# A four-layer selective-scan stack on one core: table-set blocks of ScalarE placed only behind a lift, and the next chunk's prologue re-cut around them

## Chip, cores and metric

One Trainium2 chip, one of its cores. The metric is the device time of one execution of the whole program in microseconds. The kernel before takes 22061.91 us, the median of three runs (22050.39 to 22083.94).

## What is computed

An image batch of 4 x 64 x 64 tokens with 128 channels goes through four layers. Layers 0, 1 and 3 are state-space (Mamba-like) blocks over 256 inner channels and 16 states, layer 2 is a gated block. Cut to what matters:

```python
xn = _ln(x, n1w, n1b)
xx, z = jnp.split(xn @ in_w, 2)                  # 256 inner channels each
xc = _silu(depthwise_conv3x3(xx) + conv_b)
xs = rows, columns, rows reversed, columns reversed of xc         # k = 0..3
dts, Bs, Cs = split(x_proj_w[k] @ xs[k])         # 8, 16, 16 rows
delta = jax.nn.softplus(dt_w[k] @ dts + dt_b[k])
def step(h, t):                                  # 4096 positions, per k
    h = jnp.exp(d_t[..., None] * A) * h + (d_t * x_t)[..., None] * B_t
    return h, jnp.einsum('bkdn,bkn->bkd', h, C_t)
y = sum over k of (ys[k] + Ds[k] * xs[k]), put back into row order
x = x + (_ln(y, ow, ob) * _silu(z)) @ out_w
x = x + gelu(_ln(x, n2w, n2b) @ fc1 + fc1b) @ fc2 + fc2b
```

Layer 0 uses the exact gelu, layers 1 and 3 the tanh form. All data are 32-bit floats.

## The kernel before, in words

**Turns, chunks, periods.** A turn is one batch element in one of the three state-space layers: 12 turns. In a turn each of the four directions k walks over 4096 positions in 8 chunks of 512: 32 chunks to a turn, 384 in all. The 256 channels are two halves of 128 partitions, and the 16 states come in four groups q of four; a chunk is done in 8 periods i, each for one half m and one group q (`place`, L879). There are 3072 periods, written out one behind another in the loop at L985. Nothing reorders them: the order in which Python issues instructions is the order of each engine's queue.

**One period.** DVE runs four scans over 512 positions (`scan`, L918: h = da * h + db), two with db from PSUM and two with db made by DVE itself. In the order of issue:

- ACT: two exponentials `da` for the next period (`decay`, L903), a small `save` of the last state (L928), two more `da`, another `save`, then the **lift** (L915): it copies delta*x of the next period into one of two PSUM banks `dv`, and can do so only when the scan (i, side 1, j 0) has read that bank. Then four **diagonals** (L885), 128x128 each.
- DVE: scan, scan, the two multiplications of `dv` by a row of B (L1048, L1049), scan, scan. L1048 needs the lift that was issued in the period before.
- PE: `pair_db` (L895) for the next period, eight matmuls into the one PSUM tile `dbp`, which both first scans of the running period must have read; and `add_up` (L940), which sums the products h*C of the last period in PSUM.
- POOL: `times_c` (L934): h*C of two states in one 128x1024 multiplication, twice to a period, in even periods also their sum.
- SP issues the loads of the broadcast rows of B and C (`spread`, L870), every second period.

Buffers couple the engines: three `da` tiles, four `h` and four `hc` tiles, two `dv` banks, one `dbp` tile, one PSUM bank `misc` for the prologue, one PSUM bank `gap` for the work between layers.

**The prologue of the next chunk** (`prologue`, L814) is a generator that is advanced at ten of a chunk's 16 places. Place 2i (`piece(2 * i)`, L1040) lies in the middle of period i, behind `pair_db` and ahead of the second pair of `da`. Place 2i+1 (L1066) lies at the end of the period, behind lift, diagonals and `add_up`. `PIECES` (L37) lists the places. Before the change:

- 0: loads of xs and, backwards, of xd; 3: the two matmuls of `ps_x`; 4: copy to xd, `ps_dt` of the first half (L842)
- 6: ACT adds the bias to the first half (Identity, L845), `ps_dt` of the second half
- 8: Softplus of the second half (L845) and of the first (L847), then `natural_log_exp_and_others` is loaded again (L848); PE transposes B into `ps_bt` (L851)
- 9: xd is stored to memory, `bt` copied (L856), POOL forms delta*x of the first half (L859); 10: of the second half
- 11, 12, 13: delta*x transposed to `duT` (L865, L867), half by half

**The work between layers** (`between`, L231, and `combine`, L190) is a flat list of small steps: norms, the 3x3 convolution as nine matmuls with diagonal weights, projections, Silu (L461), Gelu (L528), stores. `other(number)` (L1008) is called four times in a period: number 0 behind the first scan, 1 in the middle behind `piece(2i)`, 2 behind the third scan (ahead of the lift on ACT), 3 at the end (behind the diagonals on ACT). Each call runs steps from the front of the list while less is done than is due; what is due grows with the place, and the steps' costs are counted in matmuls (`cost`, L78; `when`, L91). A call ends behind an `empty` step or where matmul steps and others meet. In the last and the first turn a few segments are `dense`: they count steps instead.

Softplus, Silu and Gelu each lie in another set of activation tables than the exponentials and logarithms. Each such block therefore loads a set, computes, and loads `natural_log_exp_and_others` again (L254, L848). ACT does nothing else in that time.

Of the kernel before, what the change touches and what calls it, by code (L numbers as in the profile page):

```python
# [14 lines left out]
AF = mybir.ActivationFunctionType  # L15
# [18 lines left out]
PAIRED = (0, 2, 4, 6)  # L34


PIECES = (0, 3, 4, 6, 8, 9, 10, 11, 12, 13)  # L37


_VSS = [  # L40
# [37 lines left out]
def cost(step):  # L78

    return getattr(step, "matmuls", 0) or (0.05 if step is empty else 0.25)  # L80


def empty():
# [7 lines left out]
def when(place):  # L91

    chunk, place = divmod(place - 1, 4 * len(ROOM))
    i, number = divmod(place, 4)
    return chunk + (sum(ROOM[:i]) + ROOM[i] * number / 4) / sum(ROOM)
# [3 lines left out]
def vss_stack_kernel(ctx: ExitStack, tc: tile.TileContext, x: bass.AP, weights, out: bass.AP, n_batch=B, layers=(0, 1, 2, 3)):  # L99
# [6 lines left out]
    nc = tc.nc  # L106
# [19 lines left out]
    for i in layers:  # L126
# [26 lines left out]
        at, end = VSS_AT["xp"]  # L153
# [77 lines left out]
    def between(e, frm, to, psums):  # L231
# [226 lines left out]

        def silu(c, of_z):

            def run():  # L461
                part = z.wide[:, 0 if of_z else 2 : 2 if c is None else 4]
                nc.scalar.activation(part, part, AF.Silu)
                tables()

            def turn(m):
                z.down = gap1.tile([P, W, RPC], F32, tag=("cen", "sq")[m], name="down")
                nc.scalar.copy(z.down, z.wide[:, 2 + m].rearrange("p (h w) -> p w h", w=W))

            def store(m):  # L470
                to_col = lane.x_col[:, m].rearrange("p (w h) -> p w h", h=H)
                nc.sync.dma_start(out=to_col[:, :, c * RPC : (c + 1) * RPC], in_=z.down)

            S.append(run)
            if c is not None:
                S.append(lambda: turn(0))
                later(lambda: nc.sync.dma_start(out=lane.x_row[:, :, cols(c)], in_=z.wide[:, 2:4]), 2)
                rest(1)
                S.extend((lambda: store(0), lambda: turn(1)))
                rest(1)  # L480
                S.append(lambda: store(1))
            elif of_z:
                rest()
# [24 lines left out]
        def mlp(c, store):  # L508
            def fresh():
                z.t = gap1.tile([P, CH], F32, tag="t", name="t")  # L510
                return z.t

            norm(lambda: z.res, fresh, v["n2w"], v["n2b"], eps5)
            for j in range(4):

                @tensor(1)
                def up(j=j):
                    if j == 0:
                        z.wide = gap1.tile([P, 4, CH], F32, tag="wide", name="hid")
                    z.ps = bank()  # L520
                    nc.tensor.matmul(z.ps, z.fc1[:, j * P : (j + 1) * P], z.t, start=True, stop=True)  # L521

                def take(j=j):
                    nc.scalar.activation(z.wide[:, j], z.ps, AF.Identity, bias=v["fc1b"][:, j : j + 1])

                S.extend((up, take))

            def gelu():  # L528
                nc.scalar.activation(z.wide, z.wide, v["gelu"])  # L529
                tables()  # L530

            S.append(gelu)
            rest(1 + breath)
            for j in range(4):

                @tensor(1)
                def down(j=j):
                    if j == 0:
                        z.ps = bank()
                    nc.tensor.matmul(z.ps, z.fc2[:, j, :], z.wide[:, j], start=(j == 0), stop=(j == 3))  # L540

                S.append(down)

            def add():
                nc.vector.scalar_tensor_tensor(z.res, z.ps, v["fc2b"], z.res, ALU.add, ALU.add)

            rest()
            S.append(add)
            rest(1)
            if store:  # L550
                later(lambda: nc.sync.dma_start(out=lane.res[:, cols(c)], in_=z.res))
# [257 lines left out]
    def scans(pool, ring, deep, psum):  # L809
# [4 lines left out]
        def prologue(s):  # L814


            lane, v = lanes[s.e % 2], s.v
            s.xs = ring.tile([P, 2, CH], F32, tag="xs", name="xs")
            nc.sync.dma_start(out=s.xs, in_=(lane.x_col if s.columns else lane.x_row)[:, :, cols(s.c)])
            if s.first:  # L820
                s.dt = pool.tile([R, DI], F32, tag="dt", name="dt_w")
                nc.sync.dma_start(out=s.dt, in_=weights[s.layer][1][:, s.k * DI : (s.k + 1) * DI])


            s.xd_d = lane.xd[s.k % 2][s.c]
            s.xd = pool.tile([2 * NX, CH], F32, tag="xd", name="xd")
            if s.back:
                nc.sync.dma_start(out=s.xd[:NX], in_=s.xd_d[1])
            yield
            if s.back:  # L830
                yield
            else:
                ps = psum.tile([P, CH], F32, tag="misc", name="ps_x")
                for m in range(2):
                    nc.tensor.matmul(ps[: 2 * NX], v["xp"][:, s.k % 2, m, :], s.xs[:, m], start=(m == 0), stop=(m == 1))
                yield
                nc.scalar.copy(s.xd, ps[: 2 * NX])
            s.delta = pool.tile([P, 2, CH], F32, tag="delta", name="delta")
            halves = (s.flip, 1 - s.flip)
            for m in halves:  # L840
                ps = psum.tile([P, CH], F32, tag="misc", name="ps_dt")
                nc.tensor.matmul(ps, s.dt[:, m * P : (m + 1) * P], s.xd[:R], start=True, stop=True)  # L842
                yield
                func = AF.Identity if m == halves[0] else AF.Softplus
                nc.scalar.activation(s.delta[:, m], ps, func, bias=v["dtb"][:, s.k, m : m + 1])  # L845
            m = halves[0]
            nc.scalar.activation(s.delta[:, m], s.delta[:, m], AF.Softplus)  # L847
            nc.scalar.preload_act_table_set("natural_log_exp_and_others")  # L848
            ps = psum.tile([P, 4, NX], F32, tag="misc", name="ps_bt")
            for j in range(4):  # L850
                nc.tensor.transpose(ps[:, j, :], s.xd[:NX, j * P : (j + 1) * P], ident[:NX, :NX])  # L851
            yield
            if not s.back:
                nc.sync.dma_start(out=s.xd_d.rearrange("k r t -> (k r) t"), in_=s.xd)
            s.bt = pool.tile([P, 4, N], F32, tag="bt", name="bt")
            nc.scalar.copy(s.bt, ps[:, :, R : R + N])  # L856
            s.du = pool.tile([P, 2, CH], F32, tag="du", name="du")
            for m in halves:
                nc.gpsimd.tensor_mul(s.du[:, m], s.delta[:, m], s.xs[:, m])  # L859
                yield  # L860
            s.duT = pool.tile([P, 4, 2, P], F32, tag="duT", name="duT")
            for m in halves:
                ps = psum.tile([P, 4, P], F32, tag="misc", name="ps_duT")
                for j in range(4):
                    nc.tensor.transpose(ps[:, j, :], s.du[:, m, j * P : (j + 1) * P], ident)  # L865
                yield
                nc.scalar.copy(s.duT[:, :, m, :], ps)  # L867
            yield
# [116 lines left out]
        for at, (s, i) in enumerate(periods):  # L985
            then = periods[at + 1] if at + 1 < len(periods) else None
            if i == 0:
                nxt = chunks[at // 8 + 1] if at // 8 + 1 < len(chunks) else None
                if nxt:
                    pro, nxt.dt = prologue(nxt), s.dt  # L990
                s.state = pool.tile([P, 2, N], F32, tag="state", name="state") if s.first else before[0].state
                if at % (8 * per_turn) == 0:
                    segments = [
                        SimpleNamespace(todo=steps, done=0, dense=True, total=len(steps), frm=frm, to=to)

                        if to - frm <= 4 * 8
                        else SimpleNamespace(
                            todo=steps, done=0, dense=False, total=sum(map(cost, steps)), frm=when(frm), to=when(to)
                        )
                        for steps, frm, to in meanwhile(s.turn)  # L1000
                    ]
# [6 lines left out]
            def other(number):  # L1008

                place = at % (8 * per_turn) * 4 + number  # L1010
                for g in segments:
                    gone = place if g.dense else when(place)
                    while g.todo and g.done < g.total * (gone - g.frm) / (g.to - g.frm):
                        step = g.todo.pop(0)
                        g.done += 1 if g.dense else cost(step)
                        step()

                        if gone < g.to and not g.dense and (step is empty or g.todo and not alike(step, g.todo[0])):
                            break
# [152 lines left out]
```

## Time and profile before

The profiled execution took 22072.22 us; its span, from the first to the last instruction, is 22070.4 us. The rest, 1.8 us, lies outside.

| What | Value |
|---|---|
| median of three runs | 22061.91 us |
| profiled execution, its span | 22072.22 us, 22070.4 us |
| a period, the span by 3072 | 7.184 us |
| a chunk, the span by 384 | 57.5 us |
| granted TensorE clock | 0.963 |
| table loads of Softplus (L845, L848) | 384 and 384, 1283 ns each |
| table loads of Silu (L463), of Gelu (L529), back again (L254) | 168, 96, 264, 1283 ns each |
| Softplus from PSUM, Softplus in place, 128x512 | 687 and 620 ns (medians) |
| Silu 128x1024, Gelu 128x2048 | 1057 and 1910 ns (medians) |

In the profile, PE is the matmuls and PEld the weight loads of TensorE, DVE VectorE, ACT ScalarE, POOL GpSimd, SP SyncE. A line such as "DVE dv L1048 <- ACT dv L916: 730.3, 328, 7.5" says that DVE sat idle ahead of its instruction at line 1048 until ACT's at line 916 ended: 730.3 us in total, 328 times, 7.5 us at most. In the timeline, the columns are start, duration, engine, line, operation, tiles and count; idle time ahead of the group and what ended it stand in brackets.

### The profile page before, as it was taken

How to read it: one execution, taken by the hardware profiler on the slowest of the kernel's cores; microseconds unless marked ns; L12 is line 12 of the kernel's file. 1: busy time of each engine (PE TensorE's matmuls, PEld its weight loads, DVE VectorE, ACT ScalarE, POOL GpSimd, SP SyncE). 2: the span in 40 equal slices, each digit the busy share in tenths (PEclk: the TensorE clock that was granted, in tenths of full speed). 3: DMA queues.
4: the chain of work that ended last, by engine and by line, in shares of the span. 5: the costliest groups of instructions: out<-in, count | busy, mean ns of one | idle time of the engine just before them, and what ended most of it. 6: DMA issues, size and time to landing. Idle time of an engine off the chain costs nothing. (4 is left out here: it accounts for less than half of the span.)

```text
span 22070.4 us, 216982 instructions
## 1 busy us (share of the span) xinstructions
PE 19694.9 (89%) x58234; PEld 10511.8 (48%) x58234; DVE 19479.8 (88%) x20186; ACT 18587.9 (84%) x40022; POOL 19266.5 (87%) x8862
## 2 busy tenths in 40 slices
PE   7898998898889889889989988989988988898897
PEld 3444444444444444444444444444444444444443
DVE  5999999999888888899889899989988888889996
ACT  6888888888888888888888888888888888888887
POOL 5999899899888888888889888988988888889996
PEclk9999999999999999999999999999999999999999
DMA  4444444444335434434534544444443453354342
GB/s 109 147 149 146 135 144 149 136 139 151 130 131 139 142 128 140 146 133 145 144 138 144 145 141 140 141 147 134 142 149 127 137 143 137 131 140 145 140 144 101
DMA packets 2437559, 3060.10 MB, mean 139 GB/s; under 512 B 1753840, under 2 KB 1790064, under 8 KB 2238192
## 3 DMA queue, kind: packets, MB, share of 16 engines
q1 hardware_dynamic: 2436336, 3046.22, 44.4%
q8 instruction: 472, 7.73, 0.1%
q14 instruction: 751, 6.15, 0.1%
HBM read 2784.41 MB, written 261.49 MB: 138 GB/s over the span
## 5 line engine op out<-in xcount | busy, mean ns | idle before, releaser
L936 POOL TENSOR_TENSOR hc<-h,cb 128x1024 f32<-128x1024 f32 x6144 | 14399.4, 2363 | 2276.5 <-DVE h L924 1113.1
L951 PE MATMUL yp<-hc,ident 128*128 128x512 f32 x18432 | 9062.1, 618 | 688.3 <-POOL hc L938 546.8
L908 ACT ACTIVATE da<-delta,w 128x512 f32<-128x512 f32 x12288 | 8148.0, 713 | 543.5 <-DVE h L924 530.5
L924 DVE TENSOR_TENSOR_SCAN h<-da,state,dbp 128x512 f32<-128x512 f32 x5376 | 6573.3, 1262 | 818.9 <-PE dbp L899 576.0
L899 PE MATMUL dbp<-diag,duT 128*128 128x256 f32 x24576 | 6012.6, 388 | 652.4 <-DVE h L924 560.1
L924 DVE TENSOR_TENSOR_SCAN h<-da,state,dv 128x512 f32<-128x512 f32 x5376 | 6589.4, 1264 | 0.0
L899 PEld LDWEIGHTS dbp<-diag,duT 128*128 128x128 f32 x24576 | 4675.2, 193 | 2921.3 <-issue 1673.1
L951 PEld LDWEIGHTS yp<-hc,ident 128*128 128x128 f32 x18432 | 3483.6, 196 | 4999.1 <-issue 3656.8
L891 ACT ACTIVATE diag<-ident,bt 128x128 f32<-128x128 f32 x12288 | 3952.1, 402 | 0.0
L938 POOL TENSOR_TENSOR hc<-hc 128x1024 f32<-128x1024 f32 x1536 | 3624.1, 2359 | 120.4
L1048 DVE TENSOR_TENSOR dv<-dv,bb 128x512 f32<-128x512 f32 x3072 | 2088.3, 680 | 945.9 <-ACT dv L916 730.3
L916 ACT COPY dv<-du 128x512 f32<-128x512 f32 x3072 | 1799.1, 586 | 984.6 <-DVE h L924 977.1
L1049 DVE TENSOR_TENSOR dv<-dv,bb 128x512 f32<-128x512 f32 x3072 | 2118.4, 690 | 0.0
L444 PE MATMUL gap<-halo,cw 128*128 128x512 f32 x3456 | 1750.8, 604 | 5.9 <-DVE cen L281 2.2
L924 DVE TENSOR_TENSOR_SCAN h<-da,dbp 128x512 f32<-128x512 f32 x768 | 891.1, 1202 | 250.7 <-PE dbp L899 166.9
L859 POOL TENSOR_TENSOR du<-delta,xs 128x512 f32<-128x512 f32 x768 | 979.9, 1276 | 31.8 <-ACT delta L847 31.8
L842 PE MATMUL ps_dt<-xd,dt_w 8*128 8x512 f32 x1536 | 881.2, 654 | 130.2 <-ACT delta L845 78.2
L932 ACT COPY state<-h 128x2 f32<-128x2 f32 x5376 | 964.3, 179 | 0.0
L444 PEld LDWEIGHTS gap<-halo,cw 128*128 128x128 f32 x3456 | 628.1, 191 | 654.8 <-issue 617.8
L924 DVE TENSOR_TENSOR_SCAN h<-da,dv 128x512 f32<-128x512 f32 x768 | 893.8, 1204 | 0.0
L845 ACT ACTIVATE delta<-ps_dt,w 128x512 f32<-128x512 f32 x768 | 524.9, 683 | 103.0 <-PE ps_dt L842 98.2
L865 PEld LDWEIGHTS ps_duT<-ident,du 128*128 128x128 f32 x3072 | 383.7, 142 | 321.9 <-issue 255.8
(122 smaller groups left out, 11686.6 us busy)
## 6 DMA issues: line engine op xcount, KB each, us to landing
cb<-xd_d SPq DMA_DIRECT2D x1536, 1024.0 KB
bb<-xd_d SPq DMA_DIRECT2D x1536, 512.0 KB
xs<-x_row_d SPq DMA_DIRECT2D x192, 512.0 KB
xs<-x_col_d SPq DMA_DIRECT2D x192, 512.0 KB
x_col_d<-down SPq DMA_DIRECT2D x192, 256.0 KB
x_row_d<-wide SPq DMA_DIRECT2D x96, 512.0 KB
y_d<-y_sb SPq DMA_DIRECT2D x96, 512.0 KB
y<-y_d SPq DMA_DIRECT2D x96, 512.0 KB
```

Source lines behind the costliest of these rows:

```text
L444: nc.tensor.matmul(z.ps, z.cw[:, m, t, :], z.halo[c][:, dy : dy + RPC, dx : dx + W], start=(t == 0), stop=(t == 8),)
L859: nc.gpsimd.tensor_mul(s.du[:, m], s.delta[:, m], s.xs[:, m])
L891: nc.scalar.activation(s.diag[q][:, t, :, j], ident, AF.Copy, scale=s.bt[:, t, CQ * q + j : CQ * q + j + 1])
L899: nc.tensor.matmul(s.db[:, t * P : (t + 1) * P, :], s.duT[:, t, m, :], s.diag[q][:, t], start=True, stop=True)
L908: nc.scalar.activation(da[:, j], s.delta[:, m], AF.Exp, scale=s.v["a"][:, s.k, m, n : n + 1])
L916: nc.scalar.copy(dv[i % 2], s.du[:, place(s, i)[1]])
L924: nc.vector.tensor_tensor_scan(s.h[i, side][:, j, s.step], da[:, j, s.step], db[:, s.step], init, ALU.mult, ALU.add)
L936: nc.gpsimd.tensor_mul(hc, s.h[i, side], s.cb[i // 2][:, 2 * side : 2 * side + 2, :])
L938: nc.gpsimd.tensor_add(hc, hc, s.hc[i, 0])
L951: nc.tensor.matmul(getattr(s, f"yp{m}"), ident, s.hc[i, side][:, j], start=opens, stop=closes)
L1048: nc.vector.tensor_mul(db, du, s.bb[i // 2][:, 0])
L1049: nc.vector.tensor_mul(du, du, s.bb[i // 2][:, 1])
```

## The change

Four things are done at once.

- `Silu` (`run`) and `Gelu` are marked `long`. `other` holds a long step, and with it all steps behind it in its segment, until a call with number 3 (behind lift and diagonals), and never runs it in period 4. This ends when the segment's end is reached, and doesn't hold for dense segments. `end=to` gives the segment the end in places for that test.
- The prologue is cut into 11 pieces. Softplus of both halves moves from place 8 (middle of period 4) to place 9 (end of period 4).
- B's transposes move from behind the Softplus (place 8) to behind the first half's Identity (place 6, middle of period 3), and the store of xd goes with them (it was at place 9). The copy `bt` comes at place 7 (end of period 3), and `ps_dt` of the second half behind it (it was at place 6).
- delta*x comes at places 10 and 11 instead of 9 and 10, the transposes and copies of `duT` at 12, 13 and 14 instead of 11, 12 and 13.

No instruction is added or taken away. In the order of instructions of the changed program, Silu and Gelu blocks stand ahead of a lift 19 times (208 times before), the rest behind lift and diagonals.

```diff
-PIECES = (0, 3, 4, 6, 8, 9, 10, 11, 12, 13)
+PIECES = (0, 3, 4, 6, 7, 9, 10, 11, 12, 13, 14)
...
+def long(fn):
+
+    fn.long = True
+    return fn
...
+            @long
             def run():
                 part = z.wide[:, 0 if of_z else 2 : 2 if c is None else 4]
                 nc.scalar.activation(part, part, AF.Silu)
...
+            @long
             def gelu():
...
-            for m in halves:
+
+            def project(m):
                 ps = psum.tile([P, CH], F32, tag="misc", name="ps_dt")
                 nc.tensor.matmul(ps, s.dt[:, m * P : (m + 1) * P], s.xd[:R], start=True, stop=True)
-                yield
-                func = AF.Identity if m == halves[0] else AF.Softplus
+                return ps
+
+            def step_sizes(m, ps, func):
                 nc.scalar.activation(s.delta[:, m], ps, func, bias=v["dtb"][:, s.k, m : m + 1])
-            m = halves[0]
-            nc.scalar.activation(s.delta[:, m], s.delta[:, m], AF.Softplus)
-            nc.scalar.preload_act_table_set("natural_log_exp_and_others")
+
+            first, second = halves
+            ps = project(first)
+            yield
+            step_sizes(first, ps, AF.Identity)
+            if not s.back:
+                nc.sync.dma_start(out=s.xd_d.rearrange("k r t -> (k r) t"), in_=s.xd)
             ps = psum.tile([P, 4, NX], F32, tag="misc", name="ps_bt")
             for j in range(4):
                 nc.tensor.transpose(ps[:, j, :], s.xd[:NX, j * P : (j + 1) * P], ident[:NX, :NX])
             yield
-            if not s.back:
-                nc.sync.dma_start(out=s.xd_d.rearrange("k r t -> (k r) t"), in_=s.xd)
             s.bt = pool.tile([P, 4, N], F32, tag="bt", name="bt")
             nc.scalar.copy(s.bt, ps[:, :, R : R + N])
+            ps = project(second)
+            yield
+            step_sizes(second, ps, AF.Softplus)
+            nc.scalar.activation(s.delta[:, first], s.delta[:, first], AF.Softplus)
+            nc.scalar.preload_act_table_set("natural_log_exp_and_others")
+            yield
             s.du = pool.tile([P, 2, CH], F32, tag="du", name="du")
...
                             todo=steps, done=0, dense=False, end=to, total=sum(map(cost, steps)), frm=when(frm), to=when(to)
...
                     while g.todo and g.done < g.total * (gone - g.frm) / (g.to - g.frm):
+                        if not g.dense and place < g.end and hasattr(g.todo[0], "long") and (number < 3 or i == 4):
+                            break
                         step = g.todo.pop(0)
```

More of the change, by code (lines that the diff above doesn't have):

```diff
@@ L997, in scans @@
                         else SimpleNamespace(
-                            todo=steps, done=0, dense=False, total=sum(map(cost, steps)), frm=when(frm), to=when(to)
+                            todo=steps, done=0, dense=False, end=to, total=sum(map(cost, steps)), frm=when(frm), to=when(to)
                         )
```

## The prediction, made before the changed kernel was run

> **What bounds the kernel now.** I read the busy times first. No engine is full: four stand between 84 and 89%, and they stay so in every turn (a turn of layer 0, 1772 us long: PE 1599, DVE 1611, POOL 1596, ACT 1510 us).
>
> ```profile
> ## 1 busy us (share of the span) xinstructions
> PE 19694.9 (89%) x58234; PEld 10511.8 (48%) x58234; DVE 19479.8 (88%) x20186; ACT 18587.9 (84%) x40022; POOL 19266.5 (87%) x8862
> ```
>
> So the time is DVE's work, 19480 us, and 2590 us in which DVE stands still because one of the others is late. The view of waits says who is late:
>
> ```profile
> ACT dv L916 <- DVE h L924: 977.1, 1124, 4.0
> ...
> DVE h L924 <- PE dbp L899: 742.8, 557, 8.6
> ...
> DVE dv L1048 <- ACT dv L916: 730.3, 328, 7.5
> ...
> PEld ps_bt L851 <- ACT delta L845: 182.2, 121, 6.0
> ...
> PE ps_bt L851 <- ACT delta L845: 134.3, 85, 5.6
> ```
>
> The two large waits of DVE are for pair_db on PE (743 us) and for the lift on ACT (730 us). ACT itself waits for DVE 1124 times before a lift: it is mostly early, and sometimes very late. The timeline of ACT around one Softplus, and of DVE in the same stretch, shows when it is late:
>
> ```profile
> 9026.40 0.17 ACT L932 COPY state<-h 128x2 f32<-128x2 f32 x1
> 9026.58 1.28 ACT L845 ACT_TABLE_LOAD   x1
> 9027.88 0.69 ACT L845 ACTIVATE delta<-ps_dt,w 128x512 f32<-128x512 f32 x1
> 9028.46 0.62 ACT L847 ACTIVATE delta<-delta 128x512 f32<-128x512 f32 x1
> 9029.10 1.28 ACT L848 ACT_TABLE_LOAD   x1
> 9030.40 1.34 ACT L908 ACTIVATE da<-delta,w 128x512 f32<-128x512 f32 x2
> 9031.64 0.17 ACT L932 COPY state<-h 128x2 f32<-128x2 f32 x1
> 9031.72 0.62 ACT L269 ACTIVATE sq<-cen 128x512 f32<-128x512 f32 x1
> 9032.25 0.57 ACT L916 COPY dv<-du 128x512 f32<-128x512 f32 x1
> ```
>
> ```profile
> 9027.08 1.27 DVE L924 TENSOR_TENSOR_SCAN h<-da,state,dv 128x512 f32<-128x512 f32 x1
> 9028.80 2.45 DVE L924 TENSOR_TENSOR_SCAN h<-da,state,dbp 128x512 f32<-128x512 f32 x2 [0.45 <-PE dbp L899]
> 9032.86 0.70 DVE L1048 TENSOR_TENSOR dv<-dv,bb 128x512 f32<-128x512 f32 x1 [1.60 <-ACT dv L916]
> ```
>
> The block holds ACT for 3.82 us (9026.58 to 9030.40). The lift behind it starts at 9032.25; what it needs (the third scan, started 9025.31, 1.27 long) was over at 9026.6. DVE waits 1.60 us.
>
> **What the Trainium skill says.** "ScalarE: Activation LUTs", section "What ACT_TABLE_LOAD costs", gives 1283 ns for a load plus a drain of about 1380 ns. The trace agrees on the load (1283 ns in the mean of all five rows of loads: L845, L848, L463, L529, L254) and shows no room for the drain: 3.82 us is the two loads and two activations end to end. I use 3.82. "Perfetto Trace Analysis", section "Tensor Engine Instruction", calls ACT, DVE and GpSimd strict FIFOs and allows PE only to pull weight loads ahead. The trace agrees: the lift stood ready for 5.6 us behind the block, and PE's transposes of B held it for 134 us while they waited for Softplus. So what counts in this change is only who stands behind whom.
>
> **The change part by part.** Nothing is added, so only waits can change. A period is 7.18 us (22070.4 / 3072).
>
> 1. *Softplus out of the way of the lift.* I went through the 383 Softplus blocks in periods 4 (the first chunk's runs ahead of the loop) and took, for each, the wait of L1048 in period 5 that is put down to the lift, limited by how long that lift had been ready. Sum: 222 us, in 112 chunks.
>
> 2. *Silu and Gelu likewise.* A block is 3.62 us (1283 + 1057 + 1283) for Silu, 4.48 for Gelu. Of 264, 208 stand ahead of a lift now and 19 in the changed order. The same count at the next L1048: Silu 234 us in 110 of 125, Gelu 229 us in 75 of 83. The trace has 51 of these blocks behind the diagonals already, as a natural experiment. In the 16 us from such a block's start, DVE waits for ACT 1.29 us (Silu) and 1.52 us (Gelu), against 2.16 to 2.75 and 2.62 to 4.44 us in the other positions. So the gain isn't the whole wait.
>
> 3. *What comes late next.* The block now delays the exponentials and the lift of one period later, and DVE arrives there earlier. For each block I took the slack there in the trace: of the next lift (in period 6 a median of 2.27 us before L1048), of the next `da`, and of pair_db, which PE has ready a median of only 0.24 us before DVE needs it in period 5 and 0.49 in period 6. Where slack is smaller than the delay left over plus the DVE time won, the difference is lost again. Losses: Softplus 173, Silu 129, Gelu 163 us. With the lift and `da` alone as limits, they would be 286 us together. Net of 1 to 3: (222 - 173) + (234 - 129) + (229 - 163) = 220 us, or 399 us if PE keeps up.
>
> 4. *B's transposes.* They now wait for the Identity in the middle of period 3, where `ps_dt` waits for it today (78 us), and no longer for Softplus (134 us on the matmul row; the 182 us of the weight-load row is the same wait). Half of 134, 67 us, I count as won; bounds 0 and 134. `ps_dt` of the second half goes to the end of period 3, behind `bt`, which ACT reaches behind lift and diagonals. Queued behind it on PE are pair_db and add_up of period 4. The trace has no such wait; between 0 and 384 x 2.06 us = 791 us (lift 0.59, diagonals 1.28, copy 0.19 behind the third scan). The nearest row is the 78 us of `ps_dt`; I take no difference to it, because PE has the pair_db of 2 us and two add_up pairs of 1.2 us to do in that time.
>
> 5. *delta*x half a period later.* POOL starts it a median of 6.45 us (5% of chunks: 3.5 us) after Softplus ends. Softplus moves back by about two `da`, two saves, lift and diagonals, 1.32 + 0.36 + 0.59 + 1.28 = 3.6 us; delta*x by one 2.36 us product. Slack shrinks by 1.2 us: nothing, and if it did run out POOL would stop (today 31.8 us, once). Its copies to `duT` move by half a period too; they are ready 5.79 us before pair_db needs them. Nothing. On SP the store of xd passes a load of B and C rows by; it waits only for xd of period 2. Nothing.
>
> 6. *The holding itself.* A held step stops its list, which then catches up. In the changed order, the foreign matmuls between one pair_db and the next exceed 5 us (at 1.13 us for a pair) 132 times instead of 66. I price each of the 66 more at one pair: 75 us lost. Bounds 0 and 150.
>
> Sum: 220 + 67 - 75 = 212 us. The sum is made against the profiled execution (22072.22 us, of which 22070.4 are span and 1.8 lie around it); that run is 10.3 us above the median of 22061.9. Taken off the median: 21850 us, 0.96% less.
>
> **The rivals.**
>
> *PE keeps up.* If PE is late mostly because DVE and POOL are, its slack returns with theirs. Then the net is 399 + 134 - 75 = 458 us: 21600. For it: POOL waits for DVE's scans 1113 us, and PE for POOL 547. Against: 0.24 us of slack in period 5.
>
> *Nothing is left.* POOL is as busy as DVE and feeds PE; each microsecond that DVE wins turns into its wait for pair_db. Then only the 67 of step 4 stay, less the 75: 22062 - 67 + 75 = 22070. For it: Silu blocks behind the diagonals today lose 2.5 us of DVE progress between 8 us before and 24 us after, as many as the others (2.1 to 2.2). Against: Gelu blocks there lose nothing (-1.8 against +1.5 and +2.4), though they are 11.
>
> *Slower: PE waits for ACT at the end of period 3.* `ps_dt` behind `bt` blocks pair_db(5), which has 0.24 us of slack, and so DVE. It decides from 212 / 384 = 0.55 us in the mean of all chunks. At 0.85 us: 384 x 0.85 = 326 us, and 22062 - 212 + 326 = 22180. For it: that slack. Against: ACT waits at a third of its lifts, so `bt` is usually on time.
>
> That the change doesn't do what it says is excluded by the order of instructions.
>
> **How the numbers follow.** About 0.2% (44 us) is what a measurement of this kernel can tell from no change. The sum (21850, own range 21700 to 21980): 0.50. PE keeps up (21600): 0.22. Nothing left (22070): 0.11. Slower (22180): 0.17. Faster is 0.50 + 0.22 = 0.72, same 0.11, slower 0.17. The range goes from 21520 (PE keeps up, and step 6 costs nothing: 22062 - 399 - 134 = 21529) to 22100; outside lie most of the slower case and little of the fast one.
>
> **What would show it.** Step 1: waits of L1048 for the lift fall from 730 to some 300 us, and no longer peak in period 5. Step 3: DVE's waits for pair_db rise above 743, and those for `da` above the 105 of today. Step 4: no wait of `ps_bt` for a Softplus, and a new one of `ps_dt` for `bt`, under 100 us. Step 5: POOL's wait for Softplus stays under 50 us. Step 6: more waits for pair_db in stretches with convolutions. A wait of `ps_dt` for `bt` of over 200 us would make the slower case; pair_db waits below 700 the first rival.

## The result, and the profile after

The changed kernel takes 22336.4 us, the median of four runs (22325.4 to 22373.7), against 22059.2 us before (22050.4 to 22083.9): 277 us more, a ratio of 1.0125 (95% interval 1.0109 to 1.0141). The prediction was 21850 us. Its slower rival, at 22180, named one of the right places and a part of the size.

The profiled execution took 22373.65 us, of which 22371.9 are span. The first part of its page and its view of waits, in the same columns as before:

```profile
PE 19789.4 (88%) x58234; PEld 10553.0 (47%) x58234; DVE 19491.1 (87%) x20186; ACT 18608.6 (83%) x40022; POOL 19277.1 (86%) x8862
```

```profile
POOL hc L954 <- DVE h L942: 1354.6, 967, 10.5
DVE h L942 <- PE dbp L917: 1162.0, 655, 9.5
...
PEld ps_dt L851 <- ACT bt L868: 217.3, 139, 5.5
...
DVE cen L271 <- PE gap L267: 212.6, 91, 32.1
DVE dv L1068 <- ACT dv L934: 212.3, 166, 6.1
...
PE ps_dt L851 <- ACT bt L868: 96.4, 85, 4.6
...
PE ps_bt L865 <- ACT delta L855: 74.4, 47, 4.4
```

DVE works as long as before (19491 against 19480 us), so the added time is waiting. Its wait for the lift (L1068) fell from 730 to 212 us, further than forecast. Its wait for pair_db rose from 743 to 1162, its wait of `cen` for a norm's matmul from 121 to 213. By period, pair_db's wait ahead of the scans of period 5 went from 155 to 409 us: 254 of the 419 in one place. (The expectations below count such a wait by the period in which PE makes the tile, one earlier: their period 4 is period 5 here, their period 7 is period 0 of the next chunk.) There PE starts pair_db(5) a mean of 3.13 us after the scan that frees `dbp`, against 2.19 before.

One such place in the timeline of PE, and of ACT and DVE, after the change. It begins with a held Silu at the end of period 2.

```profile
1301.24 1.97 PE L917 MATMUL dbp<-diag,duT 128*128 128x256 f32 x8
1306.15 0.44 PE L865 MATMUL ps_bt<-ident,xd 40*128 40x40 f32 x4 [2.94 <-ACT delta L855]
1306.52 1.99 PE L969 MATMUL yp<-hc,ident 128*128 128x512 f32 x4
1310.26 1.12 PE L851 MATMUL ps_dt<-xd,dt_w 8*128 8x512 f32 x2 [1.75 <-ACT bt L868]
1311.31 0.80 PE L358 MATMUL gap<-ident,xt 128*128 128x128 f32 x4
1311.90 1.91 PE L969 MATMUL yp<-hc,ident 128*128 128x512 f32 x2
1313.61 2.63 PE L917 MATMUL dbp<-diag,duT 128*128 128x256 f32 x8
```

```profile
1300.74 1.06 ACT L470 ACTIVATE wide<-wide 128x1024 f32<-128x1024 f32 x1
1301.82 1.28 ACT L260 ACT_TABLE_LOAD   x1
1303.11 1.09 ACT L475 COPY down<-wide 128x512 f32<-128x512 f32 x1
1304.11 1.33 ACT L926 ACTIVATE da<-delta,w 128x512 f32<-128x512 f32 x2
1305.34 0.17 ACT L950 COPY state<-h 128x2 f32<-128x2 f32 x1
1305.42 0.67 ACT L855 ACTIVATE delta<-ps_dt,w 128x512 f32<-128x512 f32 x1
...
1308.32 0.58 ACT L934 COPY dv<-du 128x512 f32<-128x512 f32 x1
1308.83 1.28 ACT L909 ACTIVATE diag<-ident,bt 128x128 f32<-128x128 f32 x4
1310.01 0.19 ACT L868 COPY bt<-ps_bt 128x64 f32<-128x64 f32 x1
```

```profile
1304.91 2.45 DVE L942 TENSOR_TENSOR_SCAN h<-da,state,dbp 128x512 f32<-128x512 f32 x2 [0.28 <-issue]
1308.93 0.70 DVE L1068 TENSOR_TENSOR dv<-dv,bb 128x512 f32<-128x512 f32 x1 [1.56 <-ACT dv L934]
...
1316.38 2.45 DVE L942 TENSOR_TENSOR_SCAN h<-da,state,dbp 128x512 f32<-128x512 f32 x2 [3.80 <-PE dbp L917]
```

The Silu block makes the Identity late; PE holds B's transposes 2.94 us for it. The copy `bt` stands behind lift and diagonals, so `ps_dt` is held another 1.75 us. DVE has read `dbp` at 1307.4, but pair_db(5) starts at 1313.6, behind all of these, and DVE waits 3.80 us. In this place PE is also slower: from 1311.7 to 1315.1 us the trace's clock records have half of the full clock, and pair_db(5) takes 2.63 us where pair_db(4) took 1.97.

### The profile page after: what moved, and what is told of

Same layout as the page of the kernel before. It is cut to its first block, busy times and chain, and to the rows that moved or that the text cites. A ratio compares the mean times of both kernels' runs of the same rounds, so it can differ in the third digit from the quotient of the medians.

```text
span 22371.9 us, 216024 instructions
## 1 busy us (share of the span) xinstructions
PE 19789.4 (88%) x58234; PEld 10553.0 (47%) x58234; DVE 19491.1 (87%) x20186; ACT 18608.6 (83%) x40022; POOL 19277.1 (86%) x8862
## 5 line engine op out<-in xcount | busy, mean ns | idle before, releaser
L1068 DVE TENSOR_TENSOR dv<-dv,bb 128x512 f32<-128x512 f32 x3072 | 2083.6, 678 | 431.1 <-ACT dv L934 212.3
L883 PE MATMUL ps_duT<-ident,du 128*128 128x128 f32 x3072 | 477.7, 279 | 191.1 <-ACT duT L885 166.6
```

What stands on the lines that cost most here:

```text
L1068: nc.vector.tensor_mul(db, du, s.bb[i // 2][:, 0])
```

## The experiments

Times are medians. Each difference is to the kernel before on the same chip (22059 to 22066 us).

| Kernel | us | Ratio to before (95%) | Difference |
|---|---|---|---|
| changed kernel | 22336 | 1.0125 (1.0109 to 1.0141) | +277 |
| e1 hold alone | 22180 | 1.0051 (1.0038 to 1.0065) | +114 |
| e2 prologue alone | 22305 | 1.0109 (1.0095 to 1.0122) | +240 |
| e3 changed, ps_dt in the middle of period 4 | 22243 | 1.0080 (1.0067 to 1.0094) | +178 |
| e4 the same without the hold | 22145 | 1.0036 (1.0024 to 1.0049) | +80 |
| e5 hold, nothing caught up | 22527 | 1.0211 (1.0197 to 1.0225) | +463 |
| e6 e4 with delta*x as before | 22118 | 1.0023 (1.0014 to 1.0032) | +54 |
| e7 delta*x later alone | 22143 | 1.0034 (1.0022 to 1.0047) | +79 |
| e8 ps_dt at the end of period 3 alone | 22021 | 0.9982 (0.9975 to 0.9989) | -43 |
| e9 e8 with Softplus behind the lift | 22159 | 1.0041 (1.0029 to 1.0054) | +93 |
| e10 hold of Gelu alone | 22108 | 1.0020 (1.0012 to 1.0028) | +41 |
| e11 hold of Silu alone | 22127 | 1.0027 (1.0016 to 1.0038) | +61 |
| e12 lists five places later | 22103 | 1.0017 (1.0010 to 1.0023) | +36 |
| e13 e2, bt ahead of the lift | 22255 | 1.0086 (1.0073 to 1.0100) | +193 |
| e14 e12 with the hold | 22317 | 1.0114 (1.0100 to 1.0128) | +254 |
| e15 no Softplus set | 21892 | 0.9919 (0.9906 to 0.9933) | -170 |
| e16 no Silu and Gelu sets | 21519 | 0.9752 (0.9739 to 0.9765) | -543 |
| e17 Softplus by exp and ln, on e8 | 21877 | 0.9916 (0.9903 to 0.9930) | -181 |
| e18 hold, let go ahead of the lift | 22079 | 1.0009 (1.0001 to 1.0017) | +21 |

**Which part.** e1 puts only the hold into the kernel before; e2 takes only the hold out of the changed one; e3 gives the second half's `ps_dt` a piece of its own, behind pair_db(5); e4 is e3 without the hold.

```diff
-PIECES = (0, 3, 4, 6, 7, 9, 10, 11, 12, 13, 14)
+PIECES = (0, 3, 4, 6, 7, 8, 9, 10, 11, 12, 13, 14)
...
             nc.scalar.copy(s.bt, ps[:, :, R : R + N])
+            yield
             ps = project(second)
```

> e1: 

> The kernel before with the holding of Silu and Gelu alone; the prologue is as before. Theory A (the second half's ps_dt at the end of period 3, ahead of pair_db, costs the time): the hold alone gains, as the prediction's step 2 had it, about 21960 us, and DVE's wait for pair_db in period 4 stays near the 155 us of before. Theory B (what is held comes out in bursts of matmuls and late norm steps): slower than before, about 22250 us, with DVE's waits for cen and res up as in the changed kernel.

> e2: 

> The changed kernel without the hold: the re-cut prologue alone. Theory A: as slow as the changed kernel or slower, 22300 to 22450 us, pair_db waits of DVE in period 4 near 400 us. Theory B: faster than before, about 22000 us, pair_db waits in period 4 under 250 us.

> e3: 

> The changed kernel with one more yield: ps_dt of the second half stands in the middle of period 4, behind pair_db(5), instead of at the end of period 3, ahead of it; bt, Softplus and all else as changed. Theory A: DVE's pair_db wait in period 4 falls from 409 to about 150 us and the time by about 250 us, to 22080 us. Theory B: little changes, 22280 us or more.

> e4: 

> The same as the kernel with ps_dt of the second half in the middle of period 4, but without the hold. Theory A: the hold is a gain, so this is slower than the one with the hold, about 22150 us. Theory B: the hold is a loss, so this is faster than both, about 21950 us.

Neither theory holds alone. The hold loses 114 us alone and 98 on e4 (22243 - 22145), 31 on e2. `ps_dt` behind `bt` at the end of period 3 loses 160 us against the middle of period 4 without the hold (22305 - 22145), 93 with it; pair_db's wait ahead of period 5 is 436 us in e2 and 116 in e4. The time doesn't follow that wait alone: ahead of period 6 the wait is larger for it, 178 us in e4 against 107 in e2, and 177 in e3 against 92 in the changed kernel. Of the roughly 250 us that e3 was to win back, 93 came.

**The hold.** The waits of DVE in e1:

```profile
DVE h L932 <- PE dbp L907: 875.9, 604, 8.4
...
DVE dv L1058 <- ACT dv L924: 403.7, 239, 6.4
DVE cen L271 <- PE gap L267: 223.6, 91, 31.8
...
DVE h L932 <- ACT da L916: 143.9, 92, 17.0
DVE h L932 <- POOL hc L944: 138.5, 69, 5.4
...
DVE res L553 <- PE gap L548: 128.5, 22, 21.7
...
DVE res L503 <- PE gap L500: 93.1, 51, 13.4
```

The same waits before, as far as not shown yet:

```profile
DVE cen L265 <- PE gap L261: 120.8, 63, 32.0
...
DVE res L496 <- PE gap L493: 86.8, 30, 13.4
...
DVE h L924 <- POOL hc L936: 80.5, 42, 5.3
...
DVE res L545 <- PE gap L540: 36.1, 2, 21.8
```

The lift's wait falls by 327 us (730.3 - 403.7). pair_db's rises by 133, `cen`'s by 103, `res`'s (two lines) by 99, those of the scans for POOL's product and for `da` by 58 and 39. The last matmul of a norm's mean starts a median of 1.10 us before the DVE step that reads it (`cen`), against 1.82: the list's steps stand closer together.

e5 counts what is due anew after each held step (`g.total, g.done, g.frm = g.total - g.done, 0, gone`); e10 and e11 mark only Gelu or only Silu; e12 starts the lists at place 13 instead of 8, e14 does so with the hold; e18 lets go in a call with number 2, ahead of the lift:

```diff
-                        if not g.dense and place < g.end and hasattr(g.todo[0], "long") and (number < 3 or i == 4):
+                        if not g.dense and place < g.end and hasattr(g.todo[0], "long") and (number != 2 or i == 4):
```

> e5: 

> The kernel with the hold alone, and after each held step what is due is counted anew from there, so that the list is stretched and nothing is caught up. Theory A (catching up is what the hold costs: a norm's matmul and the DVE step that reads it come closer together, and DVE, which is strictly in order, waits for PE): DVE's waits of cen and res for PE fall from 446 us back to some 250, and the time from 22180 to between 21950 and 22060 us. Theory B (a block behind the diagonals is itself no better than one ahead of the lift): stays at 22150 us or more.

> e10: 

> The kernel before with Gelu alone held. Theory A (a held Gelu is the good half: blocks behind the diagonals had lost nothing in the trace of before): faster than before by 30 to 100 us. Theory B (each hold costs by what stands behind it in its list): slower by some 40 us, as 96 of the 264 holds.

> e11: 

> The kernel before with Silu alone held. Theory A: the bad half, slower than before by 100 us or more, since behind a Silu stand the copies and stores of the transposed tile and the mixer, which POOL and DVE wait for. Theory B: slower by some 70 us, as 168 of the 264 holds.

> e12: 

> The kernel before with every turn's list started five places (one and a quarter period) later and nothing else: a control of what it does to the time where the list's steps fall. If the hold's 114 us are the hold's own, this stays within 30 us of before. If it is the luck of where steps fall, this moves by 50 us or more either way.

> e14: 

> The hold alone, with every turn's list started five places later, as in the control without a hold (22103 us). If the hold costs by itself: about 22103 + 114 = 22220 us, at least 60 us above that control. If its 114 us were where steps happened to fall: within 40 us of the control.

> e18: 

> The hold alone, but a held Silu or Gelu is let go in a call with number 2, just ahead of the lift, where number 3 put it behind the diagonals (22180 us). The list is stopped as often; only the block's side of the lift differs. Theory A (the place behind the lift is worth what the prediction's step 2 said, and stopping the list costs more than that): at least 100 us above the kernel with the hold to number 3, 22280 us or more, with the lift's waits back above 900 us. Theory B (the side of the lift is worth nothing, only stopping the list counts): within 40 us of 22180.

Shifting the lists by itself moves the time by 36 us, between the two bounds of e12 (30 and 50); with the hold on top it is 214 us more (22317 - 22103). So that the hold loses isn't an accident of where steps fell. How much it loses does depend on that: 31, 98, 114 and 214 us in the four pairs that differ by the hold alone. Gelu's part and Silu's add up (41 + 61 = 102, of 114). e5 is slower still: `cen` and `res` wait less (446 down to 330 us), but the lift's wait in period 5 rises from 239 to 407; stretching the list moved everything else, and the run doesn't settle what catching up costs. e18 is the surprise, outside both of its theories. With as strict a hold, and 256 of the 264 blocks ahead of the lift, it is 100 us *faster* than e1. Its waits of DVE:

```profile
DVE dv L1058 <- ACT dv L924: 752.8, 352, 6.4
DVE h L932 <- PE dbp L907: 737.5, 578, 8.9
...
DVE cen L271 <- PE gap L267: 66.9, 33, 32.1
```

The lift waits as before, 349 us more than in e1, and pair_db, `cen` and the others wait so much less that the sum (2579 us of DVE gaps over 150 ns, 2695 in e1) is smaller. For a block and the steps that follow it in its list, the place behind the lift is the worse one. Holding as such costs little in e18: 21 us.

**The prologue's parts, one by one.** e6 drops the yield between Softplus and delta*x in e4; e7 adds a yield ahead of delta*x in the kernel before; e8 adds one ahead of the second `ps_dt` there; e9 moves e8's Softplus, with B's transposes right behind it, to the end of period 4, and both halves of delta*x to the middle of period 5; e13 copies `bt` at a new place 6.5 of e2, just ahead of the lift.

```diff
-PIECES = (0, 3, 4, 6, 8, 9, 10, 11, 12, 13)
+PIECES = (0, 3, 4, 6, 7, 8, 9, 10, 11, 12, 13)
...
             for m in halves:
+                if m != halves[0]:
+                    yield
                 ps = psum.tile([P, CH], F32, tag="misc", name="ps_dt")
```

> e6: 

> The kernel without the hold and with ps_dt in the middle of period 4, and with delta*x and the transposes to duT at the places of the kernel before (POOL's delta*x directly behind Softplus at the end of period 4). Theory A (duT's second transposes at the end of period 6 wait for ACT's copy and stand ahead of the next pair_db): DVE's pair_db wait in period 7 falls from 116 to about 30 us and the time from 22145 to about 22060 us. Theory B (Softplus behind the lift is itself the loss): the time stays near 22140 us. Either could be masked if POOL now waits for Softplus: then POOL's wait for delta rises from 45 us to several hundred and the time rises.

> e7: 

> The kernel before with delta*x, its transposes and copies half a period later and nothing else. Theory A: slower than before by 60 to 100 us, the pair_db wait in period 7 near 116 us instead of 30. Theory B: no difference, within 30 us.

> e8: 

> The kernel before with ps_dt of the second half at the end of period 3 and nothing else: B's transposes and Softplus stay in period 4, so ps_dt waits for no copy of B. Theory A (its place ahead of pair_db(5) is enough): pair_db wait in period 4 rises from 155 to 300 us or more, the time by 100 to 160 us. Theory B (the wait for the copy of B is what costs): under 50 us more.

> e9: 

> The kernel with only ps_dt of the second half at the end of period 3 (22021 us), and Softplus moved behind lift and diagonals of period 4 with B's transposes right behind it; delta*x of both halves in the middle of period 5, the rest at its places of before. Theory A (Softplus behind the lift is a small gain, and its neighbours' moves cost): the lift wait in period 5 falls from 263 to about 50 us and the time by 20 to 80 us, to 21940 to 22000. Theory B (the block only hands its delay on to the next da, norm steps and lift of period 5 and 6): 22021 us or up to 80 us more, with the waits of da and cen for ACT up by what the lift's wait falls.

> e13: 

> The re-cut prologue without the hold (22305 us), with one thing altered: ACT copies B (bt) ahead of the lift of period 3 instead of behind lift and diagonals, so that PE's ps_dt of the second half, at the end of period 3, waits less for it. Theory A (that wait, and pair_db(5) queued behind it, is what this place costs): DVE's pair_db wait in period 4 falls from 436 us to 250 or less, the time to 22100 to 22180 us. Theory B (a matmul ahead of pair_db(5) costs by its own length): time and wait stay within 40 us.

delta*x later costs 79 us alone and 27 on e6. In e7's view of waits, PE's second transposes wait for ACT's copy of the first and then stand ahead of the next chunk's pair_db, whose wait goes from 30 to 99 us. The line in e7, and the one before:

```profile
PE ps_duT L866 <- ACT duT L868: 164.8, 70, 4.6
```

```profile
PE ps_duT L865 <- ACT duT L867: 66.4, 32, 3.9
```

In e6 that wait of pair_db falls from 116 us (e4) to 46, as foreseen, but POOL's wait for Softplus rises from 45 to 130, the masking that its expectation named: 27 us is what both together leave.

e8 is a gain of 43 us, although pair_db's wait ahead of period 5 rises from 155 to 190: a matmul ahead of pair_db(5) need not cost when it waits for no copy. e13 tried to take the wait for `bt` away and moved it: ACT, now copying ahead of the lift, waits for PE's transposes, and only 50 us come back.

```profile
ACT bt L868 <- PE ps_bt L865: 534.8, 224, 13.3
```

e9 loses 138 us on e8. The lift's wait in period 5 falls from 263 to 34 us, but PE is now held by Softplus at the end of period 4 (358 us), which its expectation hadn't foreseen, and pair_db's wait rises from 779 to 986. It is no clean test of Softplus's place. e6 is nearer to one: 54 us more than before, with pair_db's wait ahead of period 6 up from 89 to 171, `da`'s from 21 to 89. But B's transposes, `bt` and `ps_dt` move in it too, so what Softplus's place costs by itself is not shown.

**Are the lift's waits time?** e15 and e16 put Relu in place of the functions and load no table.

> e15: 

> The kernel before with Relu in place of Softplus and no table loads for it: the Softplus of the step sizes is left out, and the block in period 4 shrinks from 3.82 to some 1.3 us, without its position being changed. It bounds what any place for the block can win. Theory A (DVE's waits for the lift are time, as steps 1 to 3 of the prediction had it): 100 us or more below before, as the lift's wait of 262 us in period 5 goes. Theory B (what DVE wins there PE or POOL takes back): less than 60 us below before, with pair_db waits up.

> e16: 

> The kernel before with Relu in place of Silu and of Gelu and no table loads for them: these two functions are left out, and 264 blocks shrink by 2.57 us each, without their position being changed. Theory A: 170 us or more below before (steps 2 and 3 had 171 net for moving them). Theory B: less than 80 us below, with pair_db waits up.

For the most part. Taking 2.57 us out of each of 383 blocks of Softplus (983 us of ACT) wins 170 us, out of 264 others (677 us) 543. The two waits of DVE in e15, and then in e16 (743 and 730 us before):

```profile
DVE h L923 <- PE dbp L898: 833.7, 592, 9.1
...
DVE dv L1047 <- ACT dv L915: 519.5, 249, 5.4
```

```profile
DVE h L922 <- PE dbp L897: 762.1, 570, 10.1
...
DVE dv L1046 <- ACT dv L914: 273.3, 200, 4.8
```

In e15 the lift's wait falls by 211 us and pair_db's takes 91 back; in e16 457 and 19. In the moves tried here, leaving work out of ACT won time and putting it elsewhere did not.

**The version that this points to.** delta = ln(1 + exp(x)), both functions in the set that is loaded anyway, on top of e8:

```diff
-                func = AF.Identity if m == halves[0] else AF.Softplus
-                nc.scalar.activation(s.delta[:, m], ps, func, bias=v["dtb"][:, s.k, m : m + 1])
-            m = halves[0]
-            nc.scalar.activation(s.delta[:, m], s.delta[:, m], AF.Softplus)
-            nc.scalar.preload_act_table_set("natural_log_exp_and_others")
+                nc.scalar.activation(s.delta[:, m], ps, AF.Exp, bias=v["dtb"][:, s.k, m : m + 1])
+            for m in halves[::-1]:
+                nc.scalar.activation(s.delta[:, m], s.delta[:, m], AF.Ln, bias=one)
```

> e17: 

> The kernel with ps_dt of the second half at the end of period 3 (22021 us) and Softplus made as ln(1 + exp(x)), two activations of each half from the set that is loaded anyway: no table load, and no activation more than three 128x512 ones (1.9 us) between two da where the block was 3.82 us. By the kernel that left Softplus out (170 us below before, with one activation less at period 4): 60 to 150 us below 22021, so 21870 to 21960 us. If only the table loads' total on ACT counted, the same; if the lift's waits didn't matter, 22000 or more.

21877 us, 181 us below the kernel before and 459 below the changed one. Of the 181 us, 43 are e8's; some 140 come with Softplus's new form. For these inputs x lies between -4.7 and 4.4, so exp cannot overflow. The loads of tables fall from 1296 to 528. That the two functions share a set is what "ScalarE: Activation LUTs", section "Table sets: the hidden batching unit", says of `natural_log_exp_and_others`; here 768 loads went with it.

**The granted clock.** One rival stands beside all these readings. In the traces' records TensorE's clock is either full or half. It is half for 1650 us before and 1900 us after (means 0.963 and 0.958), and neighbouring matmuls of one pair_db start 216 ns apart at full clock and 427 at half (medians). In the 6.8 us ahead of a stretch at half clock PE is idle 41% of the time before and 44% after, against 10 and 11% over the run. So where PE has waited it is often slow as well. An estimate: half of PE's busy time at half clock is lost, at most 696 us before and 779 after, 83 of the 277 us. The same estimate is 764 us in e7, 637 in e8, 656 in e18, 699 in e1 and 479 in e16. The clock may thus make up much of the small differences (e7, e8) and part of the large ones. No run separates it from the waits that come ahead of it.

## Why the prediction was wrong, by its own steps

1. *Softplus out of the way of the lift.* Right as far as it went: the lift's wait in period 5 is 27 us (262 before).
2. *Silu and Gelu.* In e1 327 of the 463 us of lift's waits that were counted went away (730 to 404), but the reading of the 51 blocks that lay behind the diagonals failed: fewer microseconds of DVE waiting *for ACT* in 16 us were taken for less waiting. e18 against e1 puts the place at a loss of 100 us. The rival "nothing is left" had the better measure for Silu, DVE's progress: no gain. For Gelu the same measure showed none lost there, on 11 blocks, and e10 lost 41 us.
3. *What comes late next.* **This step failed.** It allowed 465 of 685 us to be lost again, at three instructions of the next period, and left 220 as gain. Nothing was left: in e1 alone 327 us of the lift's waits came back as 335 of pair_db, `cen` and `res` (133 + 103 + 99), with another 97 for POOL's product and `da` (58 + 39). The lists' own steps on DVE, which wait for PE, were no part of the count. That ACT's late steps also make PE late was argued for `ps_dt` alone, in step 4.
4. *B's transposes.* The other failed step: "no difference" for `ps_dt` behind `bt`, where its place against the middle of period 4 measured 160 us without the hold and 93 with it. Its bound was 791, and the slower rival stood on it. The wait itself (96 us on the matmul row, 217 on the weight-load row, in part the same time) is smaller than what came with it, 254 us more at pair_db(5), so the sign that was to tell the slower case, over 200 us of this wait, was not reached on the matmul row. The chain Identity, transposes, copy, `ps_dt` goes four times between ACT and PE through one PSUM bank. The share of each link isn't settled, since e13 only moved the wait.
5. *delta*x later: nothing.* Wrong. POOL waits little for Softplus, about as said (51 us), but the copies' slack of 5.79 us was measured to pair_db and not to the next transposes, which need the same bank: 79 us alone, 27 in company.
6. *The holding.* Steps 2, 3 and 6 together had Silu and Gelu at -96 (-171 + 75), and e1 measured +114. The nearest to the 75 us alone is e18, a hold without the change of side: 21 us.

One way from the kernel before to the changed one goes by e6 (54), e4 (delta*x, 27 more), e2 (`ps_dt` behind `bt`, 160) and the hold (31): 272, of 277 measured. Such a chain must come to the whole, so it proves no part. In another order the shares differ: alone, the hold is 114 and delta*x 79. Open is by which link a block behind the diagonals costs more than one ahead of the lift. e18 moves the block and the list's steps behind it together.

## What to carry to other kernels

A wait that the profile put down to a block was not won here by moving the block on an in-order engine that is 84% busy beside three others as busy: count what every engine then waits for behind it, not only the next reader. Shrinking the block won (0.17 to 0.8 of the time taken off ACT here), so look first for a way to do without the table load. A step that one engine hands to another through a single bank should not stand ahead of work that has no slack, even if its own wait is small.

## What had not been expected of the hardware's timeline

A matmul pair of 1.1 us put ahead of a pair_db with 0.24 us of median slack made the kernel 43 us faster (e8). The place that it left, behind an Identity on ACT, is where it had waited: `ps_dt` for `delta` was 78 us before on the matmul row, and 12 in e8. ACT's Softplus waits more for `ps_dt` in exchange (98 us before, 305 in e8). That the old wait is the cause is argued, not shown; less time at half clock is the rival. No engine is full, yet 677 us taken off ACT in 264 places gave 543 us (e16). That ACT is nearly all of the critical path in those stretches, at 84% mean load, is a reading that no run tests; less time at half clock is part of it by the estimate above (479 us, 696 before).
